# Two batches in turn through a state space layer: the prologue cut into chunks of tokens, part of its step sizes moved beside the recurrence, and a new order of the woven chains

## The chip, the cores and the metric

The kernel runs on one core of a Trainium2 chip. The metric is the device time of one execution in microseconds (us); lower is better. A core has engines that run side by side, each through its own instructions in order: TensorE (PE, matrix products; PEld is its loading of weights), VectorE (DVE), ScalarE (ACT), GpSimd (POOL) and SyncE (SP, which here only issues transfers). They wait for each other through semaphores. SBUF is the memory on the core, PSUM holds what PE sums up.

## The reference: what is computed

Two layers over x of 2 batches × 1024 tokens × 128, all in float32 and each step with its residual. The change touches the state space layer, its neighbours and the first experts.

```python
x = x + latent_attention(layernorm(x))        # 16 heads, causal
x = x + spiking_ffn(layernorm(x))             # 0/1 spikes counted over 5 steps
x = x + state_space(layernorm(x))
x = x + spiking_ffn(layernorm(x))
x = x + linear_attention(layernorm(x))        # 4 heads of 32, its own residual inside
x = x + experts(layernorm(x))                 # 8 experts, each silu(x@wg) * (x@wu) @ wd, summed
x = x + heads_attention(layernorm(x))         # softmax over the heads' axis
x = x + experts(layernorm(x))

def state_space(u):                           # E = 256 channels, N = 16 states
    xn = u * rsqrt(mean(u * u, -1) + EPS) * norm_w
    skip = xn @ skip_w.T
    x = silu(causal_conv4(xn @ in_w.T) + conv_b)
    delta = softplus((x @ wd1.T) @ wd2.T + wd2_b)      # the step sizes
    Bt, Ct = x @ wb.T, x @ wc.T
    h[t] = exp(delta[t] * A) * h[t-1] + delta[t] * x[t] * Bt[t]    # for every channel and state
    y = sum_n(h * Ct) + x * W_D
    return u + (y * silu(skip)) @ out_w.T
```

## The kernel before, in words

`x_res` holds x in SBUF as 16 tiles of 128 tokens × 128; eight tiles are a batch, four are a chunk of 512 tokens. The program has three parts: `first_layer` (everything up to the experts of batch 0), `heads_and_experts`, and single chunks of experts before and after it (`experts_ffn`, chunk 2 and chunk 3).

In `first_layer` the order of the instructions is written out by hand: under `manual_schedule` each engine runs its instructions in the order in which the Python code issues them. The chains are generators. Every `yield` ends a step. `weave(main, side, rate)` (lines 78 to 85) issues one step of `main`, then as many of `side` as the rate has accrued; `drain` issues what is left. The stages, in order:

A. `into_space(0)` with the row maxima of batch 1's attention scores, 1.25 steps of maxima to one. A step of maxima is products into PSUM (lines 225, 234) and their reduction by DVE (line 243).

B. The recurrence of batch 0 (`loop`, lines 645 to 729) with batch 1's attention, rate 1.75. The recurrence has 32 steps, 2 channel blocks e × 16. In each, SP loads the step sizes (`s_a`, and delta·x as `s_h`, 512 KB of writing each, spread over partitions, three steps ahead), ACT makes `exp(A·delta)` (line 670), and DVE multiplies by Bx, scans, and multiplies by Cx (lines 701 to 703).

C. `out_of_space(0)` (spiking network and linear attention of batch 0), which also issues the loads of the experts' weights, with `into_space(1)` as the side, 1.2 to one. The rest of the side is drained.

D. The recurrence of batch 1 with the experts of batch 0, rate 1.4.

E. `out_of_space(1)` with the rest of those experts, 0.6 to one; the rest is drained.

`into_space(b)` is the spiking network on both chunks (9 steps a chunk, `spiking_steps`: statistics, normalizing, transposes, four products with Relu and Square, 16 matmuls into `f_py` at line 490, a count of thresholds by DVE at line 499) and then `StateSpace.prologue` (lines 553 to 643, 22 steps). The prologue takes all eight tiles at a time through two norms: `u` by DVE (line 580), `un` by ACT (line 583), transposes, `xnT`, then a convolution as four shifted products (`xc`), `rT`, the first half of the gate. Then come the sizes, for each channel block e and each chunk: a product and its bias (`s_z`, line 621), Abs and Exp on ACT (622, 623), Ln (625), a correction of rounding (626 to 630), delta and delta·x (631, 632). When both chunks of a block are done, two transfers of 512 KB write them to `s_steps` in DRAM, from where the recurrence reads them back spread. `Bx`, `Cx` and the second half of the gate stand among and behind the sizes.

`expert_steps` (lines 837 to 897) opens a chunk of 512 tokens (norm, POOL's `e_u`, transposes), in one piece for the first chunk, and then takes 32 units of one expert and one quarter of its width. A step of unit i is: two products (lines 865, 866), Silu on ACT (868), DVE's multiplication `e_h` (870), and then the output product of unit i−1 (889).

Of the kernel before, what the change touches and what calls it, by code (L numbers as in the profile page):

```python
# [9 lines left out]
F32 = mybir.dt.float32  # L10
# [9 lines left out]
P = 128  # L20
# [57 lines left out]
def weave(main, side, rate):  # L78

    due = 0.0  # L80
    for _ in main:
        due += rate
        while due >= 1.0:
            next(side, None)
            due -= 1.0

# [452 lines left out]
class StateSpace:  # L539
# [14 lines left out]
    def prologue(self, work, bank):  # L554

        self.bank = bank
        g, w, nc, b, CH = self.g, self.w, self.g.nc, self.b, self.CH
        EB = self.EB
        chunks = [(n, bass.ts(n, CH)) for n in range(2)]
        xb = g.x[:, b * TPB : (b + 1) * TPB, :]  # L560

        ln = StagedNorm(g, xb, TPB, "s")
        ln.stats(range(TPB))
        ln.root()
        yield
        ln.inverse()
        mv, rs = ln.mv, ln.rs
        rr = g.small.tile([P, TPB], F32, name="s_rr", bufs=2)
        nc.vector.tensor_mul(rr, rs, rs)
        nc.vector.tensor_mul(rr, rr, mv[:, :, 1])  # L570
        nc.scalar.activation(rr, rr, AF.Sqrt, bias=g.eps)
        nc.vector.reciprocal(rr, rr)
        yield
        u = work.tile([P, TPB, D], F32, name="s_u")
        un = work.tile([P, TPB, D], F32, name="s_un")
        xnT = work.tile([P, L + 3], F32, name="s_xnT")
        nc.vector.memset(xnT[:, 0:3], 0.0)
        for n, cols in chunks:
            for t in range(4 * n, 4 * n + 4):
                nc.vector.tensor_scalar(  # L580
                    u[:, t, :], xb[:, t, :], mv[:, t, 0:1], rs[:, t : t + 1], ALU.subtract, ALU.mult
                )
                nc.scalar.mul(un[:, t, :], u[:, t, :], rr[:, t : t + 1])
            yield
            pt = self.bank("s_pt").rearrange("p (a b) -> p a b", a=4)
            for t in range(4):
                nc.tensor.transpose(pt[:, t, :], un[:, 4 * n + t, :], g.ident)
            nc.vector.tensor_scalar(
                xnT[:, 3 + n * CH : 3 + n * CH + CH], pt.rearrange("p a b -> p (a b)"), w["norm_w"], None, ALU.mult
            )  # L590
        nc.gpsimd.tensor_add(xb, xb, u)
        yield

        gate = self.gate = self.seq.tile([P, EB, L], F32, name="s_gate")
        xc = self.xc = self.seq.tile([P, EB, L], F32, name="s_xc")
        for n, cols in chunks:
            for e in range(EB):
                ch = bass.ts(e, P)
                pm = self.project([(self.shared.inw[:, k, ch], xnT[:, n * CH + k : n * CH + k + CH]) for k in range(4)])
                nc.scalar.activation(xc[:, e, cols], pm, AF.Silu, bias=w["conv_b"][:, e, :])  # L600
                yield
        rT = work.tile([64, L], F32, name="s_rT")
        Bx = self.Bx = self.seq.tile([P, L], F32, name="s_Bx")
        Cx = self.Cx = self.seq.tile([P, L], F32, name="s_Cx")
        both = lambda name, cols: [(w[name][:, e, :], xc[:, e, cols]) for e in range(EB)]
        for n, cols in chunks:
            nc.vector.tensor_copy(rT[:, cols], self.project(both("wd1T", cols), 64))
            pm = self.project([(w["skip_wT"][:, bass.ts(0, P)], xnT[:, 3 + n * CH : 3 + n * CH + CH])])
            nc.scalar.activation(gate[:, 0, cols], pm, AF.Silu)
            yield  # L610

        steps = self.steps = [self.dram.tile([2, P, L], F32, name=f"s_steps{e}") for e in range(EB)]
        for e in range(EB):


            delta = work.tile([P, L], F32, name="s_delta")
            dtx = work.tile([P, L], F32, name="s_dtx")
            for n, cols in chunks:
                z, v, ln, rnd = [work.tile([P, CH], F32, name=name) for name in ("s_z", "s_v", "s_ln", "s_rnd")]
                pm = self.project([(w["wd2T"][:, bass.ts(e, P)], rT[:, cols])])  # L620
                nc.vector.tensor_scalar(z, pm, w["wd2_b"][:, e, :], None, ALU.add)
                nc.scalar.activation(v, z, AF.Abs)
                nc.scalar.activation(v, v, AF.Exp, scale=-1.0)
                yield
                nc.scalar.activation(ln, v, AF.Ln, bias=1.0)
                nc.vector.tensor_scalar(rnd, v, 1.0, 1.0, ALU.add, ALU.subtract)
                nc.vector.tensor_sub(rnd, v, rnd)
                if e == 0:
                    nc.vector.tensor_copy(Bx[:, cols], self.project(both("wb8T", cols)))
                nc.vector.tensor_add(ln, ln, rnd)  # L630
                nc.vector.scalar_tensor_tensor(delta[:, cols], z, 0.0, ln, ALU.max, ALU.add)
                nc.vector.tensor_mul(dtx[:, cols], delta[:, cols], xc[:, e, cols])
                yield
            nc.sync.dma_start(out=steps[e][0], in_=delta)
            nc.sync.dma_start(out=steps[e][1], in_=dtx)
            if e == 0:
                for n, cols in chunks:
                    nc.scalar.copy(Cx[:, cols], self.project(both("wc8T", cols)))
            yield
        for n, cols in chunks:  # L640
            pm = self.project([(w["skip_wT"][:, bass.ts(1, P)], xnT[:, 3 + n * CH : 3 + n * CH + CH])])
            nc.scalar.activation(gate[:, 1, cols], pm, AF.Silu)
        yield

# [192 lines left out]
def expert_steps(g, w, chunks, work, ps, ps_o):  # L837
# [24 lines left out]
    def products(n, e, fc):  # L862
        f = bass.ts(fc, P)
        pg, pu = bank("e_pg"), bank("e_pu")
        nc.tensor.matmul(pg, w["Wg"][:, e, f], opened[n], start=True, stop=True)  # L865
        nc.tensor.matmul(pu, w["Wu"][:, e, f], opened[n], start=True, stop=True)  # L866
        sg = work.tile([P, 512], F32, name="e_sg")
        nc.scalar.activation(sg, pg, AF.Silu)  # L868
        h = work.tile([P, 512], F32, name="e_h", bufs=3)
        nc.vector.tensor_mul(h, sg, pu)  # L870
        return h

    units = [(n, e, fc) for n in chunks for e in range(NE) for fc in range(FC)]
    side = opening(chunks[0]) if chunks else iter(())
    for _ in side:
        pass
    later = list(chunks[1:])
    po, held = None, None
    for i in range(len(units) + 1):
        if i % 32 == 26 and later:  # L880
            side = opening(later.pop(0))
        next(side, None)
        h = products(*units[i]) if i < len(units) else None
        if held is not None:
            n, e, fc, hp = held
            if e == 0 and fc == 0:
                po = ps_o.tile([P, 512], F32, name="e_po")
            last = e == NE - 1 and fc == FC - 1
            nc.tensor.matmul(po, w["Wd"][:, e, fc, :], hp, start=(e == 0 and fc == 0), stop=last)  # L889
            if last:  # L890
                oT = work.tile([P, 512], F32, name="e_oT", bufs=1)
                nc.scalar.copy(oT, po)
                pt = bank("e_pu").rearrange("p (a b) -> p a b", a=4)
                transpose4(g, pt, oT.rearrange("p (a b) -> p a b", a=4))
                xs = g.x[:, 4 * n : 4 * n + 4, :]
                nc.vector.tensor_add(xs, xs, pt)
        held = (*units[i], h) if i < len(units) else None
# [362 lines left out]
def first_layer(g, w, open_experts, load_expert):  # L1260
# [29 lines left out]
    def into_space(b, bank, **side):  # L1290

        with tc.tile_pool(name=f"f{b}_work", bufs=1, **side) as work:
            yield from spiking_steps(g, w, [2 * b, 2 * b + 1], work, bank)
        with tc.tile_pool(name=f"s{b}_work", bufs=1, **side) as work:
            yield from space[b].prologue(work, bank)
# [14 lines left out]

    with tc.manual_schedule(engines=ALL):
        with (
# [4 lines left out]
            weave(into_space(0, bank), maxima, 1.25)  # L1317
# [4 lines left out]
        with tc.tile_pool(name="s_work", bufs=1, reuse_waits="tile") as work:  # L1322
            weave(space[0].loop(work, bank), attend, 1.75)
        drain(attend)
        latents.close()
        open_experts()
        with ExitStack() as es:
            bank0, bank1 = banks(es, "bank0", 3, **right), banks(es, "bank1", 3, **right)
            side = into_space(1, bank1, **right)
            weave(out_of_space(0, bank0, load_experts()), side, 1.2)  # L1330
            drain(side)
        ework = pool(ends, "e_work", 2, **right)
        ps_e, ps_o = pool(ends, "e_ps", 2, space=PSUM, **right), pool(ends, "e_ps_o", 1, space=PSUM, **right)
        experts = expert_steps(g, w, [0, 1], ework, ps_e, ps_o)
        with tc.tile_pool(name="s_work", bufs=1, reuse_waits="tile") as work:
            weave(space[1].loop(work, bank), experts, 1.4)
# [116 lines left out]
```

## Time and profile before

| | us |
|---|---|
| Median of three runs (lowest, highest) | 2283.98 (2281.98, 2293.54) |
| The profiled execution | 2288.49 |
| Its span, first to last instruction | 2286.8 |
| Stage A, 287 to 459 | 172 |
| Stage B, 459 to 663 | 204 |
| Stage C, 663 to 803 | 140 |
| Stage D, 803 to 1016 | 213 |
| Stage E, 1016 to 1110 | 94 |
| `experts_ffn` of chunk 2, 1110 to 1203 | 93 |
| Heads and experts, 1203 to 2187 | 984 |
| `experts_ffn` of chunk 3, 2187 to 2287 | 100 |

Over the whole span PE is busy for 87%, DVE for 74%, ACT for 53% and POOL for 39%; the granted clock of TensorE is 0.937 of full speed. These are shares of a span with stages of different kinds, so they are read by stage: stage E, for example, says nothing about B.

How to read the profile's lines. A line of a timeline has start, duration, engine, source line, operation, output, inputs, shape and count, and in brackets the idle time before it and what ended that. A line of waits has the engine and line that waited, `<-`, what it waited for, and the total, the number and the longest in us. A line of the table by stage has the stretch, its length, and for each engine its busy time with the number of its instructions in brackets; then the granted clock, the busy share of the transfer engines and GB/s.

### The profile page before, as it was taken

What the parts mean: (1) busy time and instruction counts of PE and PEld (TensorE: products, weight loads), DVE (VectorE), ACT (ScalarE), POOL (GpSimd) and SP (SyncE); (2) the same over time, 40 slices, a digit from 0 to 9 for tenths busy, and PEclk for the clock granted to TensorE, in tenths of its full rate; (3) what the DMA queues carried; (4) which work ended last, traced back from release to release, by engine and by line L of the source; (5) the groups of instructions that cost most, each with busy time, mean ns of one, the idle gap of its engine ahead of it and who ended that gap; (6) DMA issues with size and microseconds to landing.
All of it is one profiled execution on the core that took longest, in us unless ns stands there. A gap on an engine that the chain in (4) does not pass through costs nothing. (4 is left out here: it accounts for less than half of the span.)

```text
span 2286.8 us, 36328 instructions
## 1 busy us (share of the span) xinstructions
PE 1979.8 (87%) x14832; PEld 1162.7 (51%) x14832; DVE 1691.1 (74%) x2038; ACT 1211.8 (53%) x1527; POOL 898.8 (39%) x462
## 2 busy tenths in 40 slices
PE   7679888889965668787898798988999999999999
PEld 4223343233333323334446576766777777777754
DVE  5966766898856479965323798988898898898822
ACT  1026521366723577743323675756777777776722
POOL 0012400083400000000102478888787777777720
PEclk9989987789977879999999999999999999999999
DMA  4000000196730187710000465565655555555500
GB/s 87 1 1 1 1 1 1 55 242 146 185 111 0 50 190 182 166 37 0 0 0 1 110 158 149 148 165 139 158 149 153 148 148 152 151 151 144 148 15 5
DMA packets 72646, 220.15 MB, mean 96 GB/s; under 512 B 9056, under 2 KB 19744, under 8 KB 72352
## 3 DMA queue, kind: packets, MB, share of 16 engines
q1 hardware_dynamic: 53584, 149.40, 22.0%
q0 software_dynamic: 18432, 67.12, 15.5%
q8 instruction: 116, 1.90, 0.3%
q10 hardware_dynamic: 464, 1.33, 0.3%
q14 instruction: 50, 0.41, 0.1%
HBM read 78.35 MB, written 5.24 MB: 37 GB/s over the span
## 5 line engine op out<-in xcount | busy, mean ns | idle before, releaser
L1139 POOL TENSOR_TENSOR h_a<-h_e,h_r 128x2048 f32<-128x2048 f32 x128 | 582.6, 4552 | 131.1 <-PE h_po L1145 92.2
L1105 DVE TENSOR_REDUCE h_m<-h_s 128x128 f32<-128x2048 f32 x128 | 293.2, 2291 | 70.8 <-PE h_s L1094 70.4
L1129 PE MATMUL h_pd<-h_e,ident 128*128 128x128 f32 x2048 | 261.6, 281 | 45.8 <-DMA h_e<-h_e 30.0
L1111 DVE TENSOR_TENSOR h_e<-h_s,h_m 128x2048 f32<-128x2048 f32 x128 | 292.5, 2285 | 2.3 <-DVE h_m L1105 0.6
L1114 ACT ACTIVATE h_e<-h_e 128x1024 f32<-128x1024 f32 x256 | 256.4, 1048 | 65.9 <-DVE h_e L1111 56.9
L1129 PEld LDWEIGHTS h_pd<-h_e,ident 128*128 128x128 f32 x2048 | 239.6, 192 | 89.2 <-DVE x_res L978 45.7
L950 ACT ACT_TABLE_LOAD x110 | 141.1, 1283 | 167.5 <-PE e_pgu L943 167.2
L338 POOL TENSOR_SCALAR_AFFINE_SELECT a_pT<-a_pT 128x256 f32<-128x256 f32 x120 | 135.5, 1153 | 222.2 <-ACT a_pT L335 206.1
L870 DVE TENSOR_TENSOR e_h<-e_sg,e_pu 128x512 f32<-128x512 f32 x128 | 86.8, 685 | 181.8 <-PE e_pu L866 156.5
L243 DVE TENSOR_REDUCE a_nm<-a_s 128x2 f32<-128x1024 f32 (+7 forms) x144 | 168.2, 1217 | 49.1 <-PE a_s L234 26.2
L868 ACT ACTIVATE e_sg<-e_pg 128x512 f32<-128x512 f32 x128 | 76.0, 596 | 193.3 <-PE e_pg L865 193.1
L969 PEld LDWEIGHTS h_pd<-Wd,e_h 128*128 128x128 f32 x1024 | 125.0, 191 | 95.1 <-DVE e_h L958 78.1
L889 PE MATMUL e_po<-e_h,Wd 128*128 128x512 f32 x256 | 139.4, 630 | 38.8 <-DVE e_h L870 38.7
L225 PE MATMUL a_s<-a_latT,a_qT 32*128 32x512 f32 (+3 forms) x768 | 124.8, 628 | 51.4 <-DVE a_nm L243 49.3
L335 ACT ACTIVATE a_pT<-a_st 128x1024 f32<-128x1024 f32 (+3 forms) x176 | 130.0, 792 | 63.2 <-PE a_st L321 62.8
L1094 PE MATMUL h_s<-h_qz,h_kT 32*128 32x512 f32 x1024 | 148.1, 648 | 17.1 <-DVE h_e L1111 12.1
L1124 POOL DMA_DIRECT2D h_e<-h_e x128 | 114.9, 898 | 114.8 <-DMA h_e<-h_e 49.5
L943 PE MATMUL e_pgu<-e_uT,Wg 128*128 128x256 f32 x512 | 154.9, 384 | 2.6 <-ACT h_qz L1058 2.1
L969 PE MATMUL h_pd<-Wd,e_h 128*128 128x128 f32 x1024 | 149.7, 288 | 6.6 <-DVE e_h L958 3.7
L943 PE MATMUL e_pgu<-e_uT,Wu 128*128 128x256 f32 x512 | 153.2, 381 | 0.0
L702 DVE TENSOR_TENSOR_SCAN s_h<-s_a,s_h 128x1024 f32<-128x1024 f32 x64 | 147.1, 2298 | 6.5 <-ACT s_a L670 2.6
L1114 ACT ACT_TABLE_LOAD x111 | 142.4, 1283 | 13.3 <-issue 6.5
(258 smaller groups left out, 3246.1 us busy)
## 6 DMA issues: line engine op xcount, KB each, us to landing
h_e<-h_e SPq DMA_DIRECT2D x128, 512.0 KB, 4.1
h_e<-h_e POOLq DMA_DIRECT2D x128, 512.0 KB, 4.6
s_a<-s_steps SPq DMA_DIRECT2D x64, 512.0 KB, 5.0
s_h<-s_steps SPq DMA_DIRECT2D x64, 512.0 KB, 6.5
s_steps<-s_delta SPq DMA_DIRECT2D x4, 512.0 KB, 2.6
s_steps<-s_dtx SPq DMA_DIRECT2D x4, 512.0 KB, 3.4
Wg<-in_Wg_dram SPq DMA_DIRECT2D x8, 256.0 KB, 6.0
Wu<-in_Wu_dram SPq DMA_DIRECT2D x8, 256.0 KB, 5.9
```

The source lines that it names most:

```text
L243: nc.vector.tensor_reduce(nm[:, half, i, h : h + together], s[:, :, :n], AX.X, ALU.max, negate=True)
L702: nc.vector.tensor_tensor_scan(h, a, h, 0.0, ALU.mult, ALU.add)
L889: nc.tensor.matmul(po, w["Wd"][:, e, fc, :], hp, start=(e == 0 and fc == 0), stop=last)
L943: nc.tensor.matmul(pgu[:, k, :], w[name][:, e, f], uT, start=True, stop=True)
L950: nc.scalar.activation(sg, pgu[:, 0, :], AF.Silu)
L969: nc.tensor.matmul(po[:, t, :], h[:, bass.ts(t, P)], self.w["Wd"][:, e, fc, :], start=(k == 0), stop=(k == 1))
L1094: nc.tensor.matmul(s[:, j, :].rearrange("p (k q) -> p k q", k=K), kTs[b][quad, bass.ts(kb, P)], qzs[b][quad, :, bass.ts(qb, P)], start=Tru ...
L1105: nc.vector.tensor_reduce(m, heads.rearrange("p h q -> p q h"), AX.X, ALU.max)
L1111: nc.vector.tensor_sub(e, heads, m.unsqueeze(1).to_broadcast([P, H, P]))
L1114: nc.scalar.activation(eh, eh, AF.Exp, scale=scale)
L1129: nc.tensor.matmul(pd, g.ident, e2[:, k, :], start=(k == 0), stop=(k == 7))
L1139: nc.gpsimd.tensor_mul(a, e, r.unsqueeze(1).to_broadcast([P, H, P]))
```

## The change

Two helpers: `alternate` issues one step of each of its streams in turn, `follow` one stream after another.

The prologue becomes several generators. `begin` sets up its tiles. `tokens(n)` (5 steps) takes one chunk of 512 tokens from the statistics to `rT`; the second norm's factor is worked out from the first one's statistics, so that `un` is made by DVE straight from x, and `u` by POOL. `rest(n)` (4 steps) makes `Bx`, `Cx` and both halves of the gate. `first_sizes(n)` (4 steps) makes the sizes of e=0 and the logits of e=1. `late` (6 steps) makes the sizes of e=1 and is run beside the recurrence. The sizes are written out per chunk (256 KB a transfer), e=1's from the second buffer of the tiles `s_gate` and `s_xc`.

`into_space` runs the spiking network of the first chunk, then the second chunk's in turn with `tokens(0)`, then `tokens(1)`, `first_sizes(0)` and `rest(0)` in turn, then `first_sizes(1)` and `rest(1)`: 44 steps (40 before).

`expert_steps` yields in its first opening too. Its step i now issues the multiplication of unit i−1, the products of unit i and the output product of unit i−2 (70 steps for two chunks, 65 before). This holds for `experts_ffn` as well.

In `first_layer` the rates are 1.1 in A; 1.9 in B, where the side is `late` and then the attention; in C `into_space(1)` is now the main chain and a new generator `batch0_behind` (out of space, then the experts) the side at 0.6; in D the side is `late` and then what is left of that generator at 1.6; in E its rest at 0.9.

```diff
+def alternate(*streams):
+    streams = list(streams)
+    while streams:
+        for steps in list(streams):
+            try:
+                next(steps)
+            except StopIteration:
+                streams.remove(steps)
+                continue
+            yield
+
+def follow(*streams):
+    for steps in streams:
+        yield from steps
...
+    def tokens(self, n):
...
+        mv = g.small.tile([P, 4, 2], F32, name="s_mv", bufs=2)
...
+        rs = g.small.tile([P, 2, 4], F32, name="s_rs", bufs=2)
+        nc.vector.tensor_scalar(rs[:, 0, :], mv[:, :, 1], EPS, None, ALU.add)
+        nc.vector.reciprocal(rs[:, 0, :], rs[:, 0, :])
+        nc.vector.tensor_mul(rs[:, 1, :], rs[:, 0, :], mv[:, :, 1])
+        nc.vector.tensor_scalar(rs[:, 1, :], rs[:, 1, :], EPS, None, ALU.add)
+        nc.vector.reciprocal(rs[:, 1, :], rs[:, 1, :])
+        nc.vector.tensor_mul(rs[:, 1, :], rs[:, 1, :], rs[:, 0, :])
+        nc.scalar.activation(rs, rs, AF.Sqrt)
+        yield
...
+        for t in range(4):
+            nc.vector.tensor_scalar(
+                un[:, t, :], xs[:, t, :], mv[:, t, 0:1], rs[:, 1, t : t + 1], ALU.subtract, ALU.mult
+            )
+        for t in range(4):
+            nc.gpsimd.tensor_scalar(
+                u[:, t, :], xs[:, t, :], mv[:, t, 0:1], rs[:, 0, t : t + 1], ALU.subtract, ALU.mult
+            )
+        nc.gpsimd.tensor_add(xs, xs, u)
...
+    def sizes(self, e, n, z, v, ln, delta, dtx):
...
+        nc.scalar.activation(v, z, AF.Abs)
+        nc.scalar.activation(v, v, AF.Exp, scale=-1.0)
+        yield
+        nc.scalar.activation(ln, v, AF.Ln, bias=1.0)
+        nc.vector.tensor_scalar(dtx, v, 1.0, 1.0, ALU.add, ALU.subtract)
+        nc.vector.tensor_sub(dtx, v, dtx)
+        nc.vector.tensor_add(ln, ln, dtx)
+        yield
+        nc.vector.scalar_tensor_tensor(delta, z, 0.0, ln, ALU.max, ALU.add)
+        nc.sync.dma_start(out=self.steps[e][0, :, cols], in_=delta)
+        nc.vector.tensor_mul(dtx, delta, self.xc[:, e, cols])
+        nc.sync.dma_start(out=self.steps[e][1, :, cols], in_=dtx)
+        yield
+
+    def first_sizes(self, n):
...
+        self.logits(0, n, z)
+        yield from self.sizes(0, n, z, v, ln, delta, dtx)
+        self.logits(1, n, self.late_z[:, bass.ts(n, self.CH)])
+        yield
+
+    def late(self):
+        for n in range(2):
+            cols = bass.ts(n, self.CH)
+            delta, dtx = [self.late_sizes[:, k, cols] for k in range(2)]
+            yield from self.sizes(1, n, self.late_z[:, cols], self.late_v, self.late_ln, delta, dtx)
...
     for _ in side:
-        pass
+        yield
...
-    for i in range(len(units) + 1):
-        if i % 32 == 26 and later:
+    for i in range(len(units) + 2):
+        if i % 32 == 24 and later:
             side = opening(later.pop(0))
         next(side, None)
...
+        if 0 <= i - 1 < len(units):
+            ready[i - 1] = multiply(*gated.pop(i - 1))
+        if i < len(units):
+            gated[i] = products(*units[i])
+        if 0 <= i - 2 < len(units):
+            outputs(*units[i - 2], ready.pop(i - 2))
         yield
...
+            s.begin(work, bank)
+            with tc.tile_pool(name=f"f{b}_work", bufs=1, **side) as fwork:
+                yield from spiking_steps(g, w, [2 * b], fwork, bank)
+                yield from alternate(s.tokens(0), spiking_steps(g, w, [2 * b + 1], fwork, bank))
+            yield from alternate(s.tokens(1), s.first_sizes(0), s.rest(0))
+            yield from alternate(s.first_sizes(1), s.rest(1))
...
+    def batch0_behind():
+        with ExitStack() as es:
+            bank = banks(es, "bank0", 3, **right)
+            yield
+            yield from out_of_space(0, bank, load_experts(), **right)
+        ework = pool(ends, "e_work", 2, **right)
+        ps, ps_o = pool(ends, "e_ps", 2, space=PSUM, **right), pool(ends, "e_ps_o", 1, space=PSUM, **right)
+        yield from expert_steps(g, w, [0, 1], ework, ps, ps_o)
...
-            weave(into_space(0, bank), maxima, 1.25)
+            weave(into_space(0, bank), maxima, 1.1)
...
-            weave(space[0].loop(work, bank), attend, 1.75)
-        drain(attend)
+            side = follow(space[0].late(), attend)
+            weave(space[0].loop(work, bank), side, 1.9)
+        drain(side)
...
-            side = into_space(1, bank1, **right)
-            weave(out_of_space(0, bank0, load_experts()), side, 1.2)
-            drain(side)
...
+            weave(into_space(1, banks(es, "bank1", 3, **right)), behind, 0.6)
...
-            weave(space[1].loop(work, bank), experts, 1.4)
+            side = follow(space[1].late(), behind)
+            weave(space[1].loop(work, bank), side, 1.6)
...
-            weave(out_of_space(1, banks(es, "bank", 3)), experts, 0.6)
-            drain(experts)
+            weave(out_of_space(1, banks(es, "bank", 3)), side, 0.9)
+            drain(side)
```

## The prediction

> **What bounds the kernel now.** The diff touches the five woven stages of the first layer and the expert code, so I read the table of busy time by stage first (columns: stretch, length, busy us of each engine with its instructions, granted clock, DMA share, GB/s), then the waits of each stage, then the timeline where a wait is long. I call the stages A to E, in the order of these lines:
>
> ```profile
> 287.00:459.00 172.00, 146.48 (x688) 62.69 (x688) 124.72 (x193) 44.30 (x64) 3.23 (x2) 0.77 0.07 21
> 459.00:663.00 204.00, 180.75 (x1578) 68.78 (x1579) 173.00 (x115) 114.16 (x144) 93.63 (x65) 0.92 0.76 187
> 663.00:803.00 140.00, 89.57 (x340) 49.84 (x339) 72.34 (x203) 61.37 (x98) 7.27 (x4) 0.83 0.09 29
> 803.00:1016.00 213.00, 167.66 (x454) 66.71 (x455) 188.14 (x170) 146.64 (x147) 8.47 (x8) 0.89 0.65 152
> 1016.00:1110.00 94.00, 78.94 (x271) 41.58 (x269) 44.20 (x127) 39.39 (x60) 4.35 (x3) 0.95 0.00 0
> ```
>
> A (batch 0 into the state space, beside row maxima) is shared by PE and DVE. B and D (the two recurrences) are full on DVE, 85% and 88%. C (batch 0 out, batch 1 in) is full on nothing: PE 64%, DVE 52%, ACT 44%. There two dependent chains wait for each other. E is near full on PE (84%). The waits (engine and line that waited, what for, us, times, longest) of DVE in C, of PE in A, of DVE in D and of DVE in E:
>
> ```profile
> DVE f_cnt L499 <- PE f_py L490: 27.4, 2, 13.7
> DVE s_rnd L626 <- ACT s_v L623: 9.0, 4, 2.7
> DVE s_h L701 <- DMA s_h<-s_steps: 8.3, 1, 8.3
> ```
> ```profile
> PE a_s L225 <- DVE a_nm L243: 23.3, 11, 4.3
> ```
> ```profile
> DVE e_h L870 <- PE e_pu L866: 17.4, 7, 8.5
> ```
> ```profile
> DVE e_h L870 <- ACT e_sg L868: 25.3, 10, 3.9
> ```
>
> C's largest wait is PE work of the other chain standing in front (13.7 twice), and its last is the round trip of the step sizes through memory: the last dtx is made at 793.9, the recurrence starts at 802.89.
>
> **The change by stage.** All sums are against the profiled execution: 2288.49 us, span 2286.8.
>
> *Moved work.* The sizes of e=1 leave the prologue for the first four steps of the recurrence. One 512-token chunk costs DVE 0.43+3×0.69+0.69 = 3.2 us, so 6.4 per batch. On ACT it costs, from the timeline of A, three activations of 0.63 and two loads:
>
> ```profile
> 429.76 1.28 ACT L623 ACT_TABLE_LOAD   x1
> 431.05 0.63 ACT L623 ACTIVATE s_v<-s_v 128x512 f32<-128x512 f32 x1
> 431.70 1.28 ACT L625 ACT_TABLE_LOAD   x1
> 432.99 0.63 ACT L625 ACTIVATE s_ln<-s_v 128x512 f32<-128x512 f32 x1
> ```
>
> With one load back for the recurrence's Exp: 2×(1.9+2.6+1.3) = 11.5 in B, where ACT idles 204−114 = 90. This is hidden; without that cover it would be 11.5. The Trainium skill, "ScalarE: Activation LUTs", section "Table sets: the hidden batching unit", says that Exp and Ln have a set in common and need one load together. The rows show 1.28 before each; by the rule 11.5 would be 3.8 (an estimate: no load at all, the set being in place), and the sum would not move.
>
> Each late chunk also puts two 256 KB writes on SP, waiting for DVE; the recurrence's next loads queue behind them. Loads are issued three steps (3×4.8 = 14) ahead and land in 5.0 to 6.5, so 8 us of lateness is free. The late sizes are written by step 4, their first load is issued at step 13, 40 us later.
>
> *A.* DVE loses 6.4 (late) and gains 1.4 (statistics in two halves: six small operations of 0.2 more, and a memset). The chain gets shorter: from 18+22 yields in a row to 9+9+5+3 = 26, with 44 yields in all. `un` goes from ACT to DVE and `u` from DVE to POOL, which for DVE cancels (8×0.27 each); POOL's time per chunk is 4×0.93 (the mean of its 128x128 normalizing rows in the expert code) + 1.26 (its 128x512 add) = 5.0 us. What that costs DVE no row shows exactly. Two bound it, a POOL add beside normalizing DVE instructions and the same DVE form alone:
>
> ```profile
> 731.16 4.17 DVE L73 TENSOR_SCALAR l_u<-x_res,l_mv,l_rs 128x128 f32<-128x128 f32 x8
> 731.33 2.38 POOL L591 TENSOR_TENSOR x_res<-x_res,s_u 128x1024 f32<-128x1024 f32 x1 [106.76 <-ACT s_un L583]
> ...
> 739.78 2.14 DVE L73 TENSOR_SCALAR l_un<-l_u,l_mv,l_rs 128x128 f32<-128x128 f32 x8
> ```
>
> The 4.17 is 2.14 plus 2.03, so DVE stood still for most of POOL's 2.38. At 366, however, POOL's same add (2.35) beside DVE's reductions out of PSUM cost nothing. Two chunks: 0 to 2×5.0 = 10. I take 3, as in A DVE does mostly such reductions. A rule against this edit stands in the Trainium skill, "SBUF — State Buffer": GpSimd and VectorE share a port pair as a lock, not a split of bandwidth. By that the loss would be POOL's whole duration wherever DVE uses the pair too, 10, and A would gain 7 less.
>
> PE's 23.3 of waits on reductions come from DVE being held in prologue runs; spread over more, shorter yields, a third (−7) goes. Sum −6.4+1.4+3−7 = **−9**, from −20 (two thirds of the waits go, −15.5, and POOL costs nothing) to +5 (no wait goes, POOL 10). The round trip at the end of A lies under three maxima steps and the terms after them (about 13), as now.
>
> *B.* Late DVE 6.4 on a full engine, and gaps: **+7** (+4 to +10). Attention has the same steps in the weave (52 now at 1.75, 52+6 at 1.9: 30 recurrence steps either way).
>
> *C.* Now it takes 132 us to the last dtx: batch 0's 18 spiking yields with 18×1.2 of batch 1 are 39.6 yields in the first 62 us (1.55 each), the other 32.4 take 70 (2.16). In the new order 44 yields of batch 1 lead and 26 of batch 0's 32 lie beside them; 14+22+21+8 yields by segment, at 1.55 in the first two segments, where little but spiking steps and projections stands, and 1.75 in the last two, between the two paces, as the sizes are there but half of them are gone: 22+34+37+14 = 107. By depth alone: 26 links × 3.3 (132/40) = 86. I take 102, nearer to the count since engines run in program order. Then the round trip: write 2.9 (a 256 KB DMA took 2.3, a 512 KB one 3.4) and load 8 = 11, with only a few issued steps beside it. 102+11 = 113 against 140: **−27** (−40 if depth alone counts, 89+11 = 100; −12 at today's mean of 1.82 per yield).
>
> *D.* Ten expert steps fewer (40 for 49 and the edge): DVE −10×0.69 = −7; late +6.4; batch 0's last six linear steps +4; the opening is no longer drained alone, so the 8.5 of the waits goes; other waits on e_pu −2; the edges +2. **−5** (−12 to +3). DVE stays what bounds the stage: 4.74 for a recurrence step (1.23+2.29+1.23) + 1.6×0.64 = 5.76 us, with PE at 4.6 and ACT at 4.7 for the same steps.
>
> *E.* 26 expert steps for 16. PE at full clock: batch 1's own 28.3, 24 pairs of products (four 0.43 instructions, 1.72) 41.3, 26 outputs (0.86) 22.4: 92. Before it was 28.3+25.8+13.8 = 68 in 94, at a clock of 0.95, so 22 was waiting. The later multiply removes most of the 25.3 on e_sg and of the 8.7 on e_pu. 92/0.95 + 5 = 102: **+8** (0 to +16).
>
> *The later expert chunks* run the same new order alone. They are PE-bound (87.56 of 93.00 in the first): 0±2 each. Heads: 0.
>
> Sum: −9+7−27−5+8 = −26, 2262.5. The median of the runs shown, 2283.98, is 4.5 below the profiled execution: **2258**.
>
> **Rivals.**
> 1. *Slower: the yields cost what they cost.* If in-order queues make every yield cost the same whichever chain it belongs to, A is 93 yields × 1.93 (172/89) = 180 (+8) and C 65 yields (70 less the five under the round trip) × 1.82 + 11 = 129 (−11); with B +7, D −5, E +12 that is +11. Half of POOL's largest price in both prologues (4×5.0/2 = 10) makes +21: 2309.5−4.5 = **2305**. For it: DVE and PE are in program order, and 13.7 was lost twice to PE work in front. Against it: C has no engine above 64%. It decides from C saving less than 14.
> 2. *Given back.* C saves 20 but the moved expert work lands on an E that is PE-bound throughout (+20), the rest −7: 2281.5−4.5 = **2277**. For it: PE's 84% in E. Against: 22 us of waiting there.
> 3. *A larger gain.* Depth rules: C −45 (a link of 3.1 and a round trip half covered), A −18, D −10, E +5, B +5: −63, **2221**. For it: idle engines in C. Against: A's clock of 0.77 and busy PE.
>
> That the diff doesn't do what it says is not a case: the order is written out by hand.
>
> **How the numbers follow.** A difference of 0.5% (11.4 us) is about what can be told from none. Forecast 0.61 (2236 to 2280: ±22, the half widths 13, 3, 14, 8 and 8 of the five stages added in squares), rival 1 0.14, rival 2 0.15, rival 3 0.10. Faster than 2272.6: 0.52 of the forecast, 0.05 of rival 2, all of rival 3: 0.67. Slower than 2295.4: 0.13 of rival 1. The range 2222 to 2292 leaves out rival 1 and half of rival 3.
>
> **What would show it.** C, from the last operation of batch 0's recurrence to the first of batch 1's: 113, wrong above 126; f_cnt's 27.4 below 14. D: no 8.5 on the first e_h; E: 102 with e_sg's wait below 8. A: how far DVE's rows are stretched beside POOL's four normalizing instructions decides between 3 and 10. B: 211. The late table loads on ACT must not be what a recurrence step waits for. What would make it all wrong: SP held by a late write so that a recurrence load lands late, or a chain in C that waits for batch 0's PE blocks as before.

## The result, and the profile after

The changed kernel takes 2268.1 us (median of five runs, 2264.25 to 2272.32), the kernel before 2283.98 (median of five, 2280.69 to 2293.54). The ratio is 0.9926, with a 95% interval of 0.9899 to 0.9953: faster by 17 us, between 11 and 23. The profiled execution took 2268.1, its span 2266.4.

To compare the stages in all runs I cut them at the same marks on DVE: the last addition into `x_res` of batch 0's attention, the first multiplication of each recurrence, the last addition behind each recurrence, the first aggregation of statistics of chunk 2 (`e_mv`), and its last addition. Lengths in us of the two profiled executions:

| | before | after | difference | forecast |
|---|---|---|---|---|
| up to A (same code) | 286.1 | 282.1 | -4.0 | 0 |
| A | 172.9 | 160.6 | -12.3 | -9 |
| B | 204.9 | 217.5 | +12.6 | +7 |
| C | 139.0 | 110.3 | -28.7 | -27 |
| D | 212.6 | 219.4 | +6.8 | -5 |
| E | 94.6 | 105.3 | +10.7 | +8 |
| chunk 2 | 93.9 | 92.8 | -1.1 | 0 |
| the rest (same code up to chunk 3) | 1082.8 | 1078.4 | -4.4 | 0 |

Of the 20.4 between these two executions, 8.4 lie in code that is the same. Stages A to E themselves give 10.9, where the forecast had 26. The table of busy time by stage after, A to E:

```profile
282.10:442.70 160.60, 138.46 (x688) 59.51 (x688) 121.81 (x200) 34.77 (x48) 9.65 (x11) 0.86 0.06 18
442.70:660.20 217.50, 184.17 (x1584) 67.52 (x1584) 178.06 (x125) 122.50 (x153) 82.68 (x65) 0.90 0.69 172
660.20:770.50 110.30, 81.81 (x284) 42.35 (x284) 65.53 (x192) 54.38 (x81) 11.40 (x11) 0.86 0.14 43
770.50:989.90 219.40, 154.28 (x445) 61.31 (x446) 193.18 (x179) 127.50 (x132) 17.52 (x10) 0.83 0.63 151
989.90:1095.20 105.30, 99.20 (x328) 51.02 (x326) 50.80 (x137) 44.91 (x69) 4.40 (x3) 0.98 0.00 1
```

C lost 29 us with only 7 us less work on each of PE, DVE and ACT: it was waiting that went. In B DVE is busy for 5 us more, but idle for 7.5 more too, which late sizes on a full engine don't explain. E is now PE from end to end (99.2 of 105.3, clock 0.98). The waits that answer to those shown of before (lines have moved: 745 to 747 is the recurrence step, 714 its Exp on ACT, 917 `e_h`, 912 `e_sg`, 261 the reduction in A) are DVE's in C, PE's in A, DVE's in B, in D and in E:

```profile
DVE f_cnt L517 <- PE f_py L508: 24.0, 4, 11.2
DVE s_h L745 <- DMA s_h<-s_steps: 5.6, 1, 5.6
DVE s_dtx L663 <- ACT s_v L660: 0.4, 1, 0.4
```
```profile
PE a_s L243 <- DVE a_nm L261: 12.2, 9, 4.6
```
```profile
DVE s_h L746 <- ACT s_a L714: 11.8, 8, 2.6
```
```profile
DVE e_h L917 <- PE e_pu L910: 3.7, 2, 3.2
DVE s_h L746 <- ACT s_a L714: 3.6, 1, 3.6
DVE e_h L917 <- ACT e_sg L912: 2.8, 2, 2.1
```
```profile
DVE e_h L917 <- ACT e_sg L912: 22.9, 9, 2.7
```

C's largest wait, DVE's for PE at `f_cnt`, is nearly what it was (27.4 before). What went are waits inside the sizes: the 9.0 for `s_v` is now the 0.4 at `s_dtx`, and of this line of before 1.3 is left (line 652):

```profile
DVE s_z L621 <- PE s_pm L551: 4.6, 2, 3.2
```

New are the scan's waits for `s_a` in D, and those in B have grown from this line of before to 11.8:

```profile
DVE s_h L702 <- ACT s_a L670: 2.6, 2, 2.2
```

The 8.5 at D's first `e_h` is gone, but the timeline of D shows what took its place, engine by engine:

```profile
832.84 7.18 POOL L73 TENSOR_SCALAR e_u<-x_res,e_mv,e_rs 128x128 f32<-128x128 f32 x4 [10.06 <-DVE e_rs L69]
840.64 0.59 ACT L902 COPY e_uT<-e_pg 128x512 f32<-128x512 f32 x1 [10.06 <-PE e_pg L114]
842.30 2.29 DVE L746 TENSOR_TENSOR_SCAN s_h<-s_a,s_h 128x1024 f32<-128x1024 f32 x1 [3.64 <-ACT s_a L714]
848.58 0.69 DVE L917 TENSOR_TENSOR e_h<-e_sg,e_pu 128x512 f32<-128x512 f32 x1 [2.13 <-ACT e_sg L912]
```

POOL needs 7.18 for four instructions that took 3.12 when the opening was issued alone. PE's transposes wait for them, ACT's copy waits for PE, the next `s_a` stands behind that copy in ACT's queue, and a scan waits 3.64 for it. The profile before had a sign of it: its first opening, issued alone, took 3.12, but its second one, which stood beside the recurrence, took longer:

```profile
934.81 5.35 POOL L73 TENSOR_SCALAR e_u<-x_res,e_mv,e_rs 128x128 f32<-128x128 f32 x4 [121.51 <-DVE e_rs L69]
```

### The profile page after: what moved, and what is told of

It is laid out like the page before. It is cut to its first block, busy times and chain, and to the rows that moved or that the text cites. A ratio compares the mean times of both kernels' runs of the same rounds, so it can differ in the third digit from the quotient of the medians.

```text
span 2266.4 us, 36372 instructions
## 1 busy us (share of the span) xinstructions
PE 1974.6 (87%) x14832; PEld 1157.8 (51%) x14832; DVE 1694.8 (75%) x2054; ACT 1188.3 (52%) x1497; POOL 908.5 (40%) x480
## 5 line engine op out<-in xcount | busy, mean ns | idle before, releaser
L356 POOL TENSOR_SCALAR_AFFINE_SELECT a_pT<-a_pT 128x256 f32<-128x256 f32 x120 | 125.9, 1072 | 223.3 <-ACT a_pT L353 137.5
L910 PE MATMUL e_pu<-e_uT,Wu 128*128 128x512 f32 x256 | 139.1, 626 | 19.5 <-DVE e_h L917 19.5
L243 PE MATMUL a_s<-a_latT,a_qT 32*128 32x512 f32 (+3 forms) x768 | 117.7, 590 | 41.3 <-DVE a_nm L261 39.2
```

## The experiments

Theory: the chunks and the leading chain shorten C, and the price is DVE's late sizes in B and D and PE's experts in E. Rivals: the late sizes alone make the gain; or the losses in B, D and E have other causes than the moved work. Four kernels undo or change one part of the changed kernel. One of them, e4, was faster; the other eight start from it, and it is called the base.

**e1, the sizes of e=1 in front of the recurrence again.**

```diff
             yield from alternate(s.first_sizes(1), s.rest(1))
+            yield from s.late()
...
-            weave(into_space(0, bank), maxima, 1.1)
+            weave(into_space(0, bank), maxima, 0.97)
...
-            weave(into_space(1, banks(es, "bank1", 3, **right)), behind, 0.6)
+            weave(into_space(1, banks(es, "bank1", 3, **right)), behind, 0.52)
```

(and B's side `attend` at 1.75, D's side `behind` at 1.43.)

> The changed kernel with one part undone: the sizes of e=1 stand at the end of the prologue again instead of beside the recurrence (rates of the side chains set so that the same steps fall into each stage). Theory (the late sizes only move work: what A and C save, B and D pay): against the changed kernel, C 110 to about 119 (six more yields at 1.5), A +6, B from 217 back to about 205 to 208, D -5, sum near 0: 2262 to 2272 us. Rival (the late sizes are the gain, since they shorten the chain in C): C to 130 or more, A +8, B -7, D -6, sum +15: 2283 us.

Measured: 2290.21, ratio 0.9995 (0.9983 to 1.0007). A 173.2, B 205.5, C 139.5, D 210.5, E 105.4. The theory's sum fell: C grew by 29 and all of the gain was gone. A is as long as before the change (172.9), although PE's waits for the reductions stay as low as in the changed kernel (12.2):

```profile
283.40:456.60 173.20, 147.36 (x697) 61.48 (x700) 128.09 (x210) 43.58 (x58) 9.64 (x11) 0.80 0.07 21
```
```profile
PE a_s L243 <- DVE a_nm L261: 12.9, 10, 3.5
```

Its C shows something else as well:

```profile
662.10:801.50 139.40, 92.28 (x294) 50.48 (x294) 68.71 (x201) 59.35 (x88) 11.27 (x11) 0.77 0.09 27
```

PE is busy for 92.3 with 294 instructions, where the changed kernel has 81.8 with 284, and the granted clock is 0.77 instead of 0.86. The last dtx of e=0 came 111 us after C's start (773.0 less 662.1), against 96 in the changed kernel, before any late size was due. The thinner side chain was a second edit; e5 and e10 part the two.

**e2, batch 0's chain leads in C.** The side is `into_space(1)` at 1.4 and then drained, D's side `late` and the experts at 1.6, E's rate 0.65.

> The changed kernel with one part undone: in C batch 0's chain leads again, batch 1's new prologue follows at 1.4 and what is left of it is issued alone; ten more expert steps lie in D and six fewer in E. Theory (the gain of C is that batch 1's chain leads): C from 110 back to about 130, D -4, E -9, sum +6 to +8: 2275 us. Rival (chunks and late sizes shorten C whichever chain leads): C 115 or less, D -4, E -10, sum -9: 2259 us.

Measured: 2290.93, ratio 1.0008 (0.9987 to 1.003). C 132.2 (+22), D 223.8 (+4.4), E 96.6 (-8.7). The theory's C holds; D rose rather than fell, as six expert steps took the place of six linear ones. The profiled execution (2299.97) was the slowest of the ten, and 12 of its excess over the changed kernel's lie in A and in unchanged code (4 before A, 3 in A, 5 after chunk 2).

**e3, the old order in an expert step.**

```diff
-        if 0 <= i - 1 < len(units):
-            ready[i - 1] = multiply(*gated.pop(i - 1))
-        if i < len(units):
-            gated[i] = products(*units[i])
-        if 0 <= i - 2 < len(units):
-            outputs(*units[i - 2], ready.pop(i - 2))
+        h = multiply(*products(*units[i])) if i < len(units) else None
+        if held is not None:
+            outputs(*held)
+        held = (*units[i], h) if i < len(units) else None
```

> The changed kernel with one part undone: a step of the experts issues its products, its own multiplication and the output product of the unit before, as in the kernel before. Theory (E is bound by PE's work, the order of the steps hides little): E 104 to 107, D within 4, chunks 2 and 3 within 1.5 each: 2266 to 2274 us. Rival (the new order took the 22 us of waiting out of E): E 113 to 118, D +4, sum +13: 2281 us.

Measured: 2287.34, ratio 0.9977 (0.9954 to 1.0). E 116.5 (+11.2), D 222.1 (+2.7), chunk 2 92.9 (+0.1). The rival is right: in E the new order is worth 11, though DVE's wait for `e_sg` still stands at 22.9 with it (29.2 in this run). That wait is DVE's, and DVE is idle for half of E; what went is PE's own waiting. E in this run, and PE's waits for `e_h` in E in the kernel before, in this run and in the changed kernel:

```profile
994.60:1111.10 116.50, 101.28 (x326) 51.84 (x324) 50.99 (x136) 44.91 (x69) 4.44 (x3) 0.96 0.00 1
```
```profile
PE e_po L889 <- DVE e_h L870: 9.9, 3, 6.1
PE e_po L925 <- DVE e_h L917: 10.0, 4, 5.6
PE e_pu L910 <- DVE e_h L917: 3.4, 2, 3.2
```

PE is idle for 15.2 of E here and for 6.1 in the changed kernel; the other 2 are its busy time, at a clock of 0.96 for 0.98. Where the experts run alone the order is worth nothing.

**e4, B woven at 1.75 (the base of the runs below).**

```diff
-            weave(space[0].loop(work, bank), side, 1.9)
+            weave(space[0].loop(work, bank), side, 1.75)
```

> The changed kernel with B woven at 1.75 instead of 1.9. Theory (half of B's loss comes from ACT, which stands in attention's exponentials when a scan needs its s_a; fewer attention steps to a recurrence step take that away): the waits of the scan for s_a fall from 11.8 to 4 or less, B from 217 to about 210. Rival (the same work has to be done in B in any case, and DVE is full): B 215 to 218, what the waits lose is drained at the end.

Measured: 2256.52, ratio 0.9851 (0.9827 to 0.9875), clear of the changed kernel's. B 205.2, the other stages within their spread. The table by stage for B, and DVE's wait for `s_a` there:

```profile
447.50:652.60 205.10, 179.44 (x1584) 66.84 (x1584) 178.02 (x125) 122.56 (x153) 88.63 (x65) 0.93 0.68 162
```
```profile
DVE s_h L746 <- ACT s_a L714: 4.7, 5, 1.8
```

DVE, PE and ACT do the same work as at 1.9 (178.0, 179 and 122.6) in 12.3 us less. And B is as long as before the change, with 5 us more on DVE, and as long as in e1, which has no late sizes at the same rate (205.5). So the late sizes are free in B, and all of B's loss was the rate. They aren't what `s_a` waits for either: the changed kernel's eight waits all lie after 500 us, and its late sizes are done at 468. Seven of the 12 are the waits for `s_a`; the rest I can't lay to one wait.

**e5, only batch 1's sizes in front, with the rates in C left alone.**

```diff
             weave(into_space(1, banks(es, "bank1", 3, **right)), behind, 0.6)
+            drain(space[1].late())
...
-            side = follow(space[1].late(), behind)
-            weave(space[1].loop(work, bank), side, 1.6)
+            side = behind
+            weave(space[1].loop(work, bank), side, 1.43)
```

> The kernel with B at 1.75, and only batch 1's sizes of e=1 put in front of its recurrence, issued alone after the 44 steps of the prologue (A, B and the rate in C untouched). It parts the two things that the first run of this kind mixed, the sizes themselves and the thinner side chain in C. Theory 1 (the sizes cost what their own chain takes, two times about 6): last dtx of e=0 at the same distance as with the late sizes (97), C 107 to 120, D -6, total +7: 2264 us. Theory 2 (the sizes themselves make C 139 again): C 135 or more, D -9, total +18: 2275 us.

Measured: 2259.59, ratio 0.9875 (0.9841 to 0.9909). C 120.9 (+13.5), D 208.8 (-12.4). Theory 1: batch 1's late sizes shorten C by 13.5, and D gives 12.4 of that back. In the whole time they gain 3 (5 by the ratios), and the two intervals overlap.

**e6, all eight tiles at a time, with late sizes and the leading chain.** The spiking steps of both chunks and then one generator: norm, transposes, convolutions and sizes in a row as in the kernel before (39 steps; rates 1.25 in A and 0.67 in C).

> The kernel with B at 1.75, with the prologue again on all eight tiles at a time (spiking steps of both chunks first, then norm, transposes, convolutions in a row: 39 steps, each waiting for the one before), late sizes, per-chunk writes and leading batch 1 kept. Theory (the chunks shorten the chain from 39 links to 26): C 107 to 122, A +6: total +18, 2275 us. Rival (late sizes and the leading chain carry all of the gain): C within 4, A within 3: 2253 to 2262 us.

Measured: 2281.84, ratio 0.9971 (0.9952 to 0.999). C 126.5 (+19), A 167.5 (+3 to +9). The theory holds: by the ratios the chunks are worth 27 of the time and, in e2, the leading chain 19; in C it is 19 and 22. The old way of the two norms came back with them (`u` by DVE, `un` by ACT); the runs don't price it apart.

**e7, D woven at 1.9, E at 0.55.** Ten expert steps move from E to D.

> The kernel with B at 1.75, D woven at 1.9 instead of 1.6 and E at 0.55 instead of 0.9: ten expert steps go from E to D. Theory (E is bound by PE, D by DVE: an expert step costs 2.6 in E and 0.7 in D): D +7 to +9, E from 105 to 82 to 90, total -9: 2248 us. Rival (E is bound by its chain of 32 steps and D by ACT's table loads): E 95, D +14, total +4: 2260 us.

Measured: 2249.03, ratio 0.983 (0.9803 to 0.9857). The stages D and E:

```profile
758.70:988.20 229.50, 176.62 (x497) 70.00 (x498) 198.71 (x189) 138.72 (x146) 18.26 (x10) 0.87 0.59 145
988.20:1075.50 87.30, 75.86 (x268) 40.32 (x266) 44.08 (x128) 39.15 (x59) 4.44 (x3) 0.98 0.00 0
```

D +8.3, E -18.1: an expert step costs 0.8 in D and 1.8 in E.

**e8, the experts' opening normalizes on DVE.**

```diff
         ln.inverse()
-        ln.apply(u, range(4))
+        ln.apply(u, range(4), nc.vector)
```

> The kernel with B at 1.75, where the experts' opening normalizes on DVE instead of POOL. Theory (the first opening in D holds PE and then ACT and a scan because POOL takes 7.2 us for its four instructions beside the recurrence): waits of 3.6 and 2.1 at the opening go, DVE +2.2 in D: D -4, chunks 2 and 3 -2 each as POOL's 3.1 becomes 1.1: total -8, 2249 us. Rival (PE and ACT are waiting there for DVE's own queue): D 0 to +3, total -2: 2254 us.

Measured: 2236.68, ratio 0.9779 (0.975 to 0.9807). D 212.7 (-8.5), chunk 2 89.1 (-3.6). D's line:

```profile
750.30:963.00 212.70, 152.94 (x445) 61.22 (x446) 194.89 (x187) 127.63 (x132) 4.36 (x2) 0.85 0.64 157
```

DVE does 1.7 us more than in the base and D is 8.5 shorter: the scan's 3.65 and the 2.13 for `e_sg` are both gone from its timeline. The rival fell. The gain in D is twice what was expected, since the waits for `e_pu` fell as well (5.2 in the base, 2.0 here). Of the 20 between the two medians (16 by the ratios), D and chunk 2 explain 12; in the profiled executions another 5.3 lie in A, whose code is the same (see the last section), so the opening's own worth may be nearer to 12 than to 20.

**e9, both of these.**

> The kernel with B at 1.75, with both later edits: the experts' opening normalized on DVE, D woven at 1.9 and E at 0.55. Theory (the two gains have different causes and add: -8 for the opening in D, -4 in chunk 2, about -8 for the ten steps moved): D 221, E 87, chunk 2 89, total 2228 us. Rival (both take the same waits out of D): no better than the opening alone, 2235 us.

Measured: 2233.3, ratio 0.9747 (0.9721 to 0.9772), the lowest of all and clear of both kernels: 2.5% below the kernel before. D 218.5, E 89.0, chunk 2 90.2. Against the opening alone D is +5.8 and E -16.2; the two intervals overlap, and the medians differ by 3.4 only; in the profiled executions A took 163.9 for 158.8 (see the last section).

**e10, C woven at 0.52 on the base.**

> The kernel with B at 1.75, and C woven at 0.52 instead of 0.6, as in the first run of the sizes in front: 22 of batch 0's steps lie in C and not 26. Theory (PE gets longer pauses, its granted clock falls, and C grows though it holds less work; this made that run's C 139): clock in C from 0.88 to 0.80 or less, C 115 or more. Rival (less work, shorter C; the 139 came from the sizes' place in the order): C 98 to 106, clock 0.85 to 0.9.

Measured: 2271.13, ratio 0.9919 (0.9891 to 0.9946). C 119.4 (+12) with less work in it. The table by stage for C and three of DVE's waits there:

```profile
650.00:769.40 119.40, 78.93 (x256) 41.75 (x256) 59.34 (x184) 47.98 (x72) 11.27 (x11) 0.80 0.24 73
```
```profile
DVE s_rT L634 <- PE s_pm L569: 14.4, 1, 14.4
DVE s_xc L652 <- PE s_pm L569: 10.4, 1, 10.4
DVE s_Bx L641 <- PE s_pm L569: 5.6, 1, 5.6
```

In the base those three are 0.7, 1.3 and nothing; in e1 they are 15.0, 10.4 and 5.6, so e1 has the same disorder. PE needs 78.9 for 256 instructions (79.4 for 284 in the base) at a clock of 0.80 for 0.88. So a thinner side explains 12 of e1's 29 in C, and 13.5 are the sizes. The theory gave the clock as the mechanism; the timeline shows a second one with it: ACT's copy `f_uT` of batch 0 stands behind batch 1's Sqrt, which waits 13.2 for `s_rs`, and PE then pauses 6.6 for `f_uT`. How much is the clock and how much the changed order stays open.

**e11, still more experts in D (opening on DVE, 2.15 and 0.4).**

> The opening on DVE, D woven at 2.15 and E at 0.4: nine expert steps more from E to D than at 1.9. Theory (E comes down to its own chain of 32 steps while D pays 0.7 to 0.9 a step): D +8, E -4: 2232 us, worse than 1.9. Rival (E stays bound by PE): E -15, D +8: 2222 us.

Measured: 2237.69, ratio 0.9768 (0.9737 to 0.9799). D 231.6 and E 82.7, where e9 has 218.5 and 89.0: 13 paid for 6. By these stages the theory is right that more in D loses, and D cost more than it said; the two times don't show it, as their intervals overlap (A took 158.8 here and 163.9 there).

**e12, `u` in the prologue on DVE.**

```diff
-            nc.gpsimd.tensor_scalar(
+            nc.vector.tensor_scalar(
                 u[:, t, :], xs[:, t, :], mv[:, t, 0:1], rs[:, 0, t : t + 1], ALU.subtract, ALU.mult
```

> The kernel with B at 1.75, with u in the prologue made by DVE instead of POOL. Theory (beside A's reductions POOL holds DVE for nothing, beside C's few doubled instructions for 1 to 2; DVE's own four instructions cost 1.1 a chunk): A +2, C 0, total 2258 us. Rival (POOL and DVE lock each other out for POOL's 3.1 a chunk): A -4, C -4: 2248 us.

Measured: 2254.97, ratio 0.9841 (0.982 to 0.9862). A 163.7 (164.1 in the base) with 1.9 us more on DVE; C 105.8 for 107.4. Neither a gain nor a cost of POOL's `u` that these runs can tell.

## Why the prediction was right, and which of its terms were not

The forecast of a gain, its main place and the size of that place were right: C was to lose 27 and lost 28.7. The time came out 10 above the 2258, and that near owes something to luck: the five stages were to gain 26 and gained 10.9, 8.4 of the difference of the two executions lie in unchanged code, and the range of 2222 to 2292 had room for no change at all.

In C three reasons were given together, and the runs show that each carries a part: undone one at a time, the chunks are worth 19 in C (e6), the leading chain 22 (e2) and the late sizes 13.5 (e5), 55 together where C lost 29 to 32. Undo one, and the chain has another reason to be late. In the whole time only the chunks and the leading chain are clear of noise. Counted from C's start, the last dtx of e=0 came after 110.6 before and 96.1 after, e=1's sizes took another 19.5 before and nothing after, and the way from there to the recurrence grew from 9.0 to 14.2. The forecast had 102 and 11 for the 96.1 and the 14.2, two misses that nearly cancel. Its sign for the mechanism, `f_cnt`'s wait below 14, failed at 24.0: PE work of the other chain still stands in front. And its count, a time for every yield, isn't what sets C's length by itself: e10 issues four yields fewer and is 12 longer.

- **A, -9 for -12.3: near, by other terms.** The line of PE's waits for the reductions fell by 11 instead of 7, but others came (4.5 for the maxima's terms, 3.8 for `s_un`), and PE's whole idle time fell by 3.4 only, from 25.5 to 22.1. The other 8.0 is that the same 688 instructions took 138.5 instead of 146.5, at a granted clock of 0.86 for 0.77, a term that the sum doesn't have. e1 shows that the waits for the reductions don't set A's length: with them at 12.9 A took 173.2. What it put back, the sizes of e=1 (and a rate of 0.97), takes all of A's gain away. And A with the same instructions varies by 5.3 from run to run (last section), more than the 3.3 between forecast and result. POOL's price, taken as 3, was 0: A's timeline has no stretched row, and e12 finds no difference. The Trainium skill, "SBUF — State Buffer", section "Who interferes with whom", says that a VectorE instruction with at most one input in SBUF, outside the doubled modes, doesn't contend with GpSimd; A's reductions out of PSUM agree with it (1.21 to 1.23 for one of 128x1024, beside POOL's `s_u` and away from it). The price of 10 that the prediction worked out from the lock left this condition aside.
- **B, +7 for +12.6: the term that failed in its cause.** "Late DVE 6.4 on a full engine" was not what B paid. e4 has the same 178 us on DVE and B at 205.2. The term missed the other half of the change there: the rate of 1.9 puts ACT's exponentials of the attention ahead of `s_a` (at 602.55 two of them take 1.94, `s_a` follows at 604.38, and the scan has waited 2.60 for it).
- **D, -5 for +6.8: the term that failed in its sign.** The DVE part was nearly right (-6.6 for the multiplications, +6.4, +3.9). "The opening is no longer drained alone, so the 8.5 goes" was wrong: DVE's idle time in D, which was to fall by 10, rose from 24.9 to 26.2. Two thirds of the wait came back as a chain through POOL, PE and ACT, 3.6 and 2.1 on DVE. e8 shows the cause: POOL's normalizing beside the recurrence, 8.5 in D. The late sizes, put at 6.4, cost 12.4 (e5, at a rate of 1.43 for 1.6): 7.3 is DVE's work and 5.1 its idle time. Two scans were stretched by 1.8 together, beside POOL's additions of batch 0's linear attention. The waits for `s_py` and `s_po` at the end of the recurrence grew too (4.4 before, 10.5 now), but e8 has 10.4 of them and the base 5.8, so they don't go with D's length.
- **E, +8 for +10.7.** PE's count was near (92 at full clock, 97 at the 0.95 taken; 99.2 busy at 0.98). The sign named for it, `e_sg`'s wait below 8, failed: it stood at 22.9, a wait of an engine that E isn't short of. What the new order of an expert step removed is seen on PE: 9.9 waiting for `e_h` before, 3.4 after. e3 prices it at 11.
- **The later chunks, 0 for -1.1**, as e3 confirms (92.8 and 92.9).

Rival 1 (every yield costs the same) is refuted in C, but e10 shows what was true in it: the engines' fixed order makes C's length hang on which step stands before which, 12 us for a rate of 0.52 or 0.6. Rival 2's place was right (E is PE-bound throughout), at half its price. A and C gained 41 us in the profiled execution, and B, D and E gave back 30. Of these 30 the rate in B (12) and POOL in the opening (8.5) were not needed.

## What to carry to other kernels

When steps are moved beside another chain, ask what the new ratio of the weave puts into the other engines' queues, not only what the moved steps cost on the full engine: in B the steps were free and the ratio cost 12 us. A chain that is issued in small steps beside a full engine must not pass through an engine that this one slows down; four short instructions on POOL cost 8.5 us that way, and on DVE the same four take 1.1. A wait counts only on the engine that the stage is short of: in E PE's idle time fell by 9 of the 11 us that the new order is worth, while DVE's wait for `e_sg`, on which the forecast had set its sign, still stood at 22.9.

## What the runs showed of the hardware

POOL's four 128x128 instructions took 3.12 alone or beside reductions out of PSUM, and 7.18 and 5.98 at the two openings beside the recurrence, whose instructions have two inputs in SBUF. In e3 the second opening fell into a pause of DVE in the recurrence and took 3.11. One scan beside a POOL add took 3.17 for 2.29. In C a 0.42 instruction of DVE (line 663) took 2.29 beside POOL's 2.35 add.

A has the same instructions in ten of these runs, yet two lengths: 158.8 in three, 163.9 to 164.1 in six (160.6 in the changed kernel's own profile). e8 and e4 in A:

```profile
281.00:439.80 158.80, 136.21 (x688) 58.92 (x688) 121.85 (x199) 34.78 (x48) 9.69 (x11) 0.87 0.06 17
```
```profile
283.40:447.50 164.10, 141.89 (x688) 60.58 (x688) 121.94 (x200) 34.78 (x48) 9.65 (x11) 0.85 0.06 17
```

Every engine does the same; PE is busy for 5.7 us more at a lower granted clock, and A is 5.3 longer. PE's waits for the reductions are 12.6 and 12.2. In stretches of 10 us the clock falls to about 0.5 around PE's pauses in both, but comes back at different places: after the second pause e8 is at 0.96 in the next stretch (from 371 on), and e4 stays between 0.63 and 0.68 for three (363 to 393). The Trainium skill, "TensorE: Matmul & The Clock Gate", section "Part 1: The HAM clock gate (the "warmup" mystery)", says that the clock follows the activity in a free-running window, so that the same kernel can find different phases of it; the two lengths agree with that, and no run here varies the phase on purpose.
